# Causal attention with two products a head, one maximum over two banks, and banks handed out by hand

## The chip, the cores and the metric

The kernel runs on one core of one Trainium2 chip. The metric is the device time of one execution in microseconds (us). Engines in the text are those of the profile: PE (matrix products) with PEld (its weight loads), DVE (vector), ACT (scalar functions), POOL, and SP, which here only starts transfers. Each engine works through its own queue in order.

## The reference, cut to what matters

A sequence of 2048 rows of 128 numbers goes through four layers, each added to its own input. The first is a linear recurrence with a gate, the second a choice of one expert out of eight, the third causal attention with 16 heads of 8 numbers each, and the fourth six rounds of windowed attention and a gated feed-forward layer. The change touches the third:

```python
qkv = x @ W_qkv + b_qkv                       # x is normalised first
q, k, v = ...                                 # 16 heads of 8 numbers
scores = einsum('bhqd,bhkd->bhqk', q, k) * D ** (-0.5)
scores = where(tril, scores, -inf)
probs = softmax(scores, axis=-1)
out = einsum('bhqk,bhkd->bhqd', probs, v)
return out @ W_o + b_o
```

## The kernel before

**Layout.** Rows are worked in 4 groups of 512 (`NG`, `GW`), heads in 4 groups of 4 (`NGRP`). A head has a stripe of 32 partitions: its 8 numbers stand there three times, and the last 8 partitions carry other things (below). Four heads fill the 128 partitions, so that their products, 32 partitions high each, can run side by side on PE.

**Precision.** The scores are computed from bfloat16 pieces whose sum is nearly the float32 number. q is cut into three bfloat16 pieces (`project`, L617): the rounded value, the rounded rest, and the rest of that. They are the three planes of the tile `qT`. The key (`keys`, L468) is cut into three pieces as well, but these stand in one plane `kT`, one piece in each of the three 8-partition parts of the stripe. One product of a 32-partition stripe sums a piece of q times all three pieces of k; three products, accumulated in one PSUM bank (512 float32 per partition), give the score (`products`, L630).

**What a key costs.** For each of the 4 row groups and 4 head groups (16 times), `keys` runs a matmul into bank `pk`, ACT `k` (the rounded key), DVE `krest` (the rest), POOL `k` (a product with a 0/1 column) and POOL `kT` (a difference). `project` runs, for each of 16 blocks, a matmul into `pq`, ACT `qT`, DVE `qrest`, POOL `qT` as a cast and POOL `qT` as a difference.

**Two passes.** Softmax needs each row's maximum first. `maxima` (L636) computes the scores with rows on the partitions, up to 512 keys at a time, for two heads in a *half*: the products go into two banks, in the last chunk a small matmul adds the causal mask, and DVE takes the maximum of each bank (`mx`). When a block (one head group, 512 rows) is done, POOL cuts the negated maxima into pieces, and PE and DVE put them into the spare partitions of plane 0 of `qT` (`finish`, L682). Against ones in the key's spare partitions, they subtract the maximum inside the product. `attend` (L703) then computes the scores again, with keys on the partitions, and ACT takes the exponential straight from the bank into `ex`; on the diagonal POOL zeroes the future (`whole`, L746), and PE multiplies with the values into `av`.

**Order.** `attention` (L898) pairs a unit of `attend` for block b with a unit of `maxima` for a later block. A unit is four heads and is done in two halves; a half issues the products of two maxima heads and two attention heads, then the two exponentials, then PE's `av` products of an earlier unit (`weigh_due`), then the two maxima. Where the maxima are behind, `catch_up` (L883) puts a unit of maxima alone, four heads at once; where they are far enough ahead, a unit of `attend` goes alone. All this is order of issue. `InOrder` (L57) pins every PE, DVE, ACT and POOL instruction behind the one issued before it on that engine:

```python
def run(*args, **kw):
    return self._tc.keep_in_program_order(call(*args, **kw))
```

**Banks.** PSUM has 8 banks: one for `av`, seven for everything else, as seven buffers of one pool (L560). A new tile waits until its buffer's last reader is done.

**The front.** Before and beside the first blocks, `front` (L485) runs the recurrence, the experts and the keys. They are generators, merged by written due times (`Merge`, L72). For the experts DVE writes `own`, the rows of one expert, eight times a row group, and PE multiplies each (`py`); before every layer a normalisation goes DVE, POOL (`ln_r`), DVE (`ln_h`), PE (`ln_pt`), ACT (`hT`). `keys` is called for one head group (L466) or for three in a row, and issues all of a key without a break.

Of the kernel before, what the change touches and what calls it, by code (L numbers as in the profile page):

```python
# [93 lines left out]

class Kernel:
# [27 lines left out]
    def norm_transposed(self, pool, psum, x, g, hT):  # L123

        mv = pool.tile([P, G, 2], F32, name="ln_mv")
        for j in range(G):
            st = pool.tile([P, 6], F32, name="ln_st")
            self.dve.bn_stats(st, x[:, g * G + j, :])
            self.dve.bn_aggr(mv[:, j, :], st)
        var = pool.tile([P, G], F32, name="ln_var")  # L130
        self.dve.tensor_scalar_add(var, mv[:, :, 1], EPS)
        r = pool.tile([P, G], F32, name="ln_r")
        self.rsqrt(r, var)
        yield 3.2
# [7 lines left out]
        self.act.copy(hT, pt)  # L142
        yield 2.3
# [54 lines left out]
    def load3(self, w):  # L198
        nc, a = self.nc, self.a
        wqk = w.tile([P, 2, NGRP, P], F32, name="wqk")  # L200
        nc.sync.dma_start(wqk, a["wqk1"])
        bqk = w.tile([P, 4, NGRP], F32, name="bqk")
# [57 lines left out]
    def ssm_inputs(self, pool, psum, x, g, into, f1, gate, xsT):  # L260

        w4, vec, bt, ct = self.w1
        cpg = GW // CL
        hT = pool.tile([P, GW], F32, name="hT", tag="t")
        yield from self.norm_transposed(pool, psum, x, g, hT)
        px = psum.tile([P, GW], F32, name="px", tag="b")
        self.pe.matmul(px, lhsT=w4[:, 0, :], rhs=hT, start=True, stop=True)
        xs_g = xsT[:, g * GW : (g + 1) * GW]
        self.dve.tensor_copy(xs_g, px)
        yield 3.0  # L270
        for c in range(2):
            pb = psum.tile([P, GW], F32, name="pb", tag="b")
            self.pe.matmul(pb, lhsT=bt[:, c, :], rhs=xs_g, start=True, stop=True)
            fg = f1[:, :, c, g * cpg : (g + 1) * cpg].rearrange("p l k -> p k l")
            pb = pb.rearrange("p (k l) -> p k l", l=CL)
            if c == 0:
                self.act.activation(fg, pb, AF.Copy, scale=into)
            else:
                self.dve.tensor_scalar_mul(fg, pb, into)
# [7 lines left out]
        self.act.activation(gate[:, g * G : (g + 1) * G, :], pg, AF.Silu)  # L287

# [53 lines left out]
    def ssm_out(self, pool, psum, x, g, gate, po, u):  # L342
# [11 lines left out]
        for j in range(G):  # L354
            self.act.activation(sq[:, j, :], po[:, j, :], AF.Square, accum_out=ss[:, j : j + 1])
        yield 0.9
# [8 lines left out]
        self.act.copy(uT, pu)  # L365
        yield 1.0
# [6 lines left out]
        for j in range(G):  # L373
            xt = x[:, g * G + j, :]
            self.dve.scalar_tensor_tensor(xt, pr[:, j, :], r[:, j : j + 1], xt, ALU.mult, ALU.add)

    def experts(self, pool, psum, x, g):
# [27 lines left out]
        for j in range(G):  # L407
            act.activation(
                ex[:, j, :], pl[:, j, :], AF.Exp, bias=mx[:, 1, j : j + 1], accum_out=prob[:, j : j + 1]
            )  # L410
        idi = pool.tile([P, G], I32, name="idi")
# [19 lines left out]
        for e in range(EXPERTS):  # L431
            yield 0.7
            own = pool.tile([P, GW], F32, name="own", bufs=4)
            dve.scalar_tensor_tensor(own, pi, float(e), hT, ALU.is_equal, ALU.mult)
            yield 0.4
# [8 lines left out]
        for j in range(G):  # L444
            act.activation(y[:, j, :], py[:, j, :], AF.Relu, scale=prob[:, j : j + 1])
        yield 1.7
# [5 lines left out]
    def keys_values(self, pool, psum, x, g, hT3, kT, va):  # L452
# [11 lines left out]
        )  # L464
        yield 1.3
        yield from self.keys(pool, psum, g, hT3, kT, [0])  # L466

    def keys(self, split, psum, g, hT3, kT, grps):  # L468
        wqk, bqk, wv, wo = self.w3
        hg = hT3[:, g * GW : (g + 1) * GW]  # L470
        for grp in grps:
# [8 lines left out]
            self.dve.scalar_tensor_tensor(rest, pk, bqk[:, 1, grp : grp + 1], one, ALU.add, ALU.subtract)  # L480
            self.gps.tensor_scalar_mul(two, rest, bqk[:, 3, 1:2])
            self.gps.tensor_tensor(kT[:, grp, g * GW : (g + 1) * GW], rest, two, ALU.subtract)
# [71 lines left out]
    def stages123(self, x, x3):  # L554
        nc, tc, a = self.nc, self.tc, self.a
        with ExitStack() as ctx:
# [4 lines left out]
            psum_s = ctx.enter_context(tc.tile_pool(name="s3s", bufs=7, space=PSUM))  # L561
            pe, dve, act, gps = self.pe, self.dve, self.act, self.gps

            class banks:
                @staticmethod
                def tile(shape, dtype, name, tag=None):
                    return psum_s.tile(shape, dtype, name=name, tag="sc")

# [3 lines left out]
            make_kT = lambda: keep.tile([P, NGRP, T], BF16, name="kT3", tag="kT3")  # L572
# [44 lines left out]
            def project(b):  # L617
                grp, qc = blocks[b]
                q = qs[b] = pool.tile([P, 3, GW], BF16, name="qT3", bufs=4)
                pq = bank("pq")  # L620
                pe.matmul(
                    pq, lhsT=wqk[:, 0, grp, :], rhs=hT[:, qc * GW : (qc + 1) * GW], start=True, stop=True
                )
                rest = pool.tile([P, GW], F32, name="qrest")
                act.activation(q[:, 0], pq, AF.Identity, bias=bqk[:, 0, grp : grp + 1])
                dve.scalar_tensor_tensor(rest, pq, bqk[:, 0, grp : grp + 1], q[:, 0], ALU.add, ALU.subtract)
                gps.tensor_copy(q[:, 1], rest)
                gps.tensor_tensor(q[:, 2], rest, q[:, 1], ALU.subtract)

            def products(heads):  # L630
                for i in range(3):
                    for product in heads:
                        product(i)


            def maxima(b):  # L636
# [6 lines left out]
                for j in range(G):  # L643
# [5 lines left out]
                    def part(pr, ch, qt=qt, mx=mx, chunks=chunks, j=j):  # L649
                        c, wd = chunks[ch]  # L650
                        n = len(chunks)
                        scs, heads = [], []
                        for h in (2 * pr, 2 * pr + 1):
                            sc = bank("sc1")
                            scs.append((h, sc))

                            def product(i, r=slice(32 * h, 32 * h + 32), sc=sc):
                                pe.matmul(
                                    sc[:, :wd], lhsT=q[r, i, j * P : (j + 1) * P], rhs=kT[r, grp, c : c + wd],
                                    start=i == 0, stop=i == 2 and ch < n - 1,  # L660
# [21 lines left out]
                def finish():  # L682
# [3 lines left out]
                    dve.tensor_tensor(q[:, 0], q[:, 0], pt, ALU.add)  # L686

# [15 lines left out]
            def attend(b):  # L703
# [15 lines left out]
                for kt in range(last + 1):  # L719
# [3 lines left out]
                    def part(pr, kt=kt, lo=lo):  # L723
# [4 lines left out]
                        for h in (2 * pr, 2 * pr + 1):  # L728
# [3 lines left out]
                            def product(i, r=slice(32 * h, 32 * h + 32), sc=sc):  # L732
                                pe.matmul(
                                    sc[:, lo:], lhsT=kT[r, grp, kt * P : (kt + 1) * P],
                                    rhs=q[r, i, lo:], start=i == 0, stop=i == 2,
# [4 lines left out]
                        def rest():  # L740
                            for h, sc in scs:
                                act.activation(ex[:, h, lo:], sc[:, lo:], AF.Exp)

# [22 lines left out]
                def close():  # L766
# [8 lines left out]
                    def back():  # L775
                        pt = bank("pta").rearrange("p (j h s) -> p j h s", h=4, s=32)
# [13 lines left out]
                        )  # L790
                        if grp == (NGRP - 1 if qc != left else NGRP - 2):
# [4 lines left out]
            def out_a(g):  # L796
# [4 lines left out]
                act.copy(aoT, pt)  # L801

                def out_b():
# [7 lines left out]
                    dve.tensor_tensor(xg, x[:, g * G : (g + 1) * G, :], po, ALU.add)  # L811
                    if g == left:
# [15 lines left out]
            def norm(g, mv, r):  # L828
# [8 lines left out]
                for i in range(2):  # L837
                    rs = slice(64 * i, 64 * i + 64)
                    act.copy(self.s4_in[rs, g * GW + i : (g + 1) * GW + i], pt[rs])

# [709 lines left out]
def _layouts(x):  # L1550
# [18 lines left out]
    bqk = np.zeros((4, NGRP, 4, 32), f)  # L1569
    for i in range(3):  # L1570
# [3 lines left out]
        if i:  # L1574
# [3 lines left out]
    bqk[1, ..., 3 * HD1 : 3 * HD1 + 3] = 1.0  # L1578
    got["wqk1"] = wqk.reshape(P, 2, NGRP, P)
    got["bqk1"] = bqk.reshape(4, NGRP, P).transpose(2, 0, 1)  # L1580
# [35 lines left out]
```

## Time and profile before

| | us |
|---|---|
| median of 3 runs (2319.01 to 2319.07) | 2319.02 |
| the profiled execution, its own time | 2321.57 |
| its span | 2319.6 |

Stages of the span, in us of busy time. They are cut at about where the first score products start (190.6), shortly after the last key is done (268.5), and where the fourth layer begins (783):

| from - to | length | PE | DVE | ACT | POOL | PE clock |
|---|---|---|---|---|---|---|
| 0 - 140 | 140 | 89.53 | 96.78 | 44.58 | 44.74 | 0.82 |
| 140 - 194 | 54 | 39.77 | 34.19 | 13.71 | 28.02 | 0.84 |
| 194 - 275 | 81 | 66.90 | 56.62 | 27.54 | 43.62 | 0.85 |
| 275 - 640 | 365 | 334.63 | 275.47 | 210.94 | 45.38 | 0.97 |
| 640 - 783 | 143 | 128.83 | 78.30 | 91.54 | 22.94 | 0.96 |
| 783 - 2319.6 | 1536.6 | 1468.36 | 1332.99 | 1249.83 | 1206.81 | 0.98 |

How to read it: an engine is busy while one of its instructions runs; matmuls overlap one another, so PE's busy time also covers the fill and drain of a product. The clock is the share of full speed that PE was granted. Nearly every instruction carries the line of the helper `InOrder` (L67), so groups are told apart by their tiles: `sc<-kT,qT` is a product of `maxima` (key columns stream through), `sc<-qT,kT` one of `attend`. Names are those of the output and inputs, and `x12` counts instructions. A float32 matmul appears as two instructions. In the chain of waits each line is a stretch of the work that ended last: its start, its length, and what ran.

### The profile page before, as it was taken

How to read it: one execution, taken by the hardware profiler on the slowest of the kernel's cores; microseconds unless marked ns; L12 is line 12 of the kernel's file. 1: busy time of each engine (PE TensorE's matmuls, PEld its weight loads, DVE VectorE, ACT ScalarE, POOL GpSimd, SP SyncE). 2: the span in 40 equal slices, each digit the busy share in tenths (PEclk: the TensorE clock that was granted, in tenths of full speed). 3: DMA queues.
4: the chain of work that ended last, by engine and by line, in shares of the span. 5: the costliest groups of instructions: out<-in, count | busy, mean ns of one | idle time of the engine just before them, and what ended most of it. 6: DMA issues, size and time to landing. Idle time of an engine off the chain costs nothing.

```text
span 2319.6 us, 62002 instructions
## 1 busy us (share of the span) xinstructions
PE 2128.0 (92%) x26188; PEld 1233.9 (53%) x26188; DVE 1874.4 (81%) x2808; ACT 1638.1 (71%) x3219; POOL 1391.5 (60%) x2122
## 2 busy tenths in 40 slices
PE   4777988999999779999999999999999999999997
PEld 2654323333333346666666666666666666666654
DVE  6667677777766489999899988998999899998963
ACT  3322445566656578888888888888888888888881
POOL 4235411100011489988788878887888887887850
PEclk8787989999999979999999999999999999999998
DMA  2000000000000100000000000000000000000000
GB/s 78 1 1 1 2 2 2 2 2 2 2 2 2 68 2 20 4 20 2 20 11 23 2 20 11 22 2 20 11 22 2 20 9 3 2 2 2 2 6 14
DMA packets 14135, 25.38 MB, mean 11 GB/s; under 512 B 1657, under 2 KB 10530, under 8 KB 13090
## 3 DMA queue, kind: packets, MB, share of 16 engines
q1 hardware_dynamic: 13276, 20.97, 2.8%
q8 instruction: 206, 3.38, 0.6%
q14 instruction: 71, 0.58, 0.1%
q10 hardware_dynamic: 582, 0.46, 0.1%
HBM read 20.37 MB, written 1.05 MB: 9 GB/s over the span
## 4 chain that ended last, share of the span: by engine, by line
PE 64%; DVE 19%; ACT 8%; issue 4%; POOL 3%; DMA 0%; DVEq 0%; POOLq 0%; ACTq 0%; SPq 0%
PE big L67 45%; PE sc L67 9%; PE av L67 5%; DVE mx L67 4%; DVE rot_a L67 3%; DVE rot_b L67 2%; ACT sq L67 2%; ACT L67 1%; ACT ge L67 1%; DVE at L67 1%; ACT zs L67 1%; PE py L67 1%; ACT ex L67 1%; DVE act L67 1%; DVE ss L67 1%
## 5 line engine op out<-in xcount | busy, mean ns | idle before, releaser
L67 ACT ACTIVATE sm<-sm,mx,rn 128x64 f32<-128x64 f32 x1536 | 519.2, 430 | 0.3
L67 DVE TENSOR_REDUCE mx<-sc 128x1 f32<-128x512 f32 (+3 forms) x640 | 355.0, 604 | 125.5 <-PE sc L67 118.6
L67 POOL TENSOR_TENSOR rot_a<-rot_a,rot_b 128x1024 f32<-128x1024 f32 x192 | 454.6, 2368 | 0.1
L67 ACT ACTIVATE ex<-sc 128x512 f32<-128x512 f32 (+3 forms) x640 | 302.6, 536 | 204.1 <-PE sc L67 200.8
L67 PE MATMUL big<-wqk,s 128*128 128x512 f32 x768 | 369.2, 604 | 15.0 <-DVE rot_b L67 10.2
L67 PE MATMUL big<-zs,vo 128*128 128x256 f32 x1536 | 366.9, 382 | 0.3 <-ACT zs L67 0.3
L67 PEld LDWEIGHTS big<-zs,vo 128*128 128x128 f32 x1536 | 280.6, 190 | 88.3 <-issue 56.8
L67 DVE TENSOR_TENSOR rot_a<-big,tab 128x1024 f32<-128x1024 f32 x192 | 233.5, 1216 | 47.1 <-ACT sq L67 36.4
L67 PE MATMUL sc<-qT,kT 32*128 32x512 bf16 (+3 forms) x1920 | 248.4, 351 | 24.6 <-DVE mx L67 16.3
L67 ACT ACTIVATE sq<-big 128x1024 f32<-128x1024 f32 x192 | 197.4, 1028 | 76.0 <-PE big L67 46.1
L67 ACT COPY zs<-big 128x1024 f32<-128x1024 f32 x192 | 192.3, 1006 | 64.3 <-PE big L67 64.3
L67 PE MATMUL sc<-kT,qT 32*128 32x512 bf16 (+3 forms) x1920 | 232.4, 359 | 1.6 <-DVE krest L67 0.5
L67 DVE TENSOR_REDUCE ss<-sq 128x16 f32<-128x1024 f32 x192 | 229.8, 1198 | 1.4
L67 DVE TENSOR_TENSOR rot_b<-big,tab 128x1024 f32<-128x1024 f32 x192 | 230.0, 1198 | 0.3 <-POOL rot_a L67 0.3
L67 PE MATMUL big<-at,xw 32*128 32x512 f32 x1536 | 206.2, 624 | 3.9 <-DVE rot_b L67 1.7
L67 PEld LDWEIGHTS big<-wqk,s 128*128 128x128 f32 x768 | 135.7, 192 | 137.0 <-issue 125.6
L67 PE MATMUL big<-ident,rot_a 128*128 128x128 f32 x1536 | 198.9, 276 | 6.2 <-POOL rot_a L67 3.6
L67 PEld LDWEIGHTS big<-ident,rot_a 128*128 128x128 f32 x1536 | 176.6, 142 | 50.3 <-issue 23.5
L67 POOL TENSOR_SCALAR_AFFINE_SELECT ex<-ex 128x512 f32<-128x512 f32 x64 | 40.8, 638 | 269.8 <-ACT ex L67 269.6
L67 POOL TENSOR_TENSOR sm<-sm,su 128x1024 f32<-128x1024 f32 x96 | 183.1, 1907 | 23.4 <-DVE su L67 22.2
L67 PE MATMUL av<-ex,va 128*32 128x256 f32 (+1 forms) x2432 | 180.5, 377 | 5.0 <-POOL ex L67 3.7
L67 POOL TENSOR_TENSOR rot_a<-rot_a,rn 128x1024 f32<-128x1024 f32 x96 | 182.7, 1904 | 0.2
(236 smaller groups left out, 3342.4 us busy)
## 6 DMA issues: line engine op xcount, KB each, us to landing
wqk<-in_L_ffn_Wqkv SPq DMA_DIRECT2D x12, 512.0 KB, 4.9
wvo<-in_wvo SPq DMA_DIRECT2D x6, 1024.0 KB, 4.9
w<-in_L_ffn_W SPq DMA_DIRECT2D x6, 341.0 KB, 7.5
x<-in_L_attn_hidden_states SPq DMA_DIRECT2D x4, 256.0 KB, 4.3
out<-act SPq DMA_DIRECT2D x4, 256.0 KB, 2.3
rot<-in_rot SPq DMA_DIRECT2D x1, 960.0 KB, 7.0
w<-in_L_ffn_W SPq DMA_DIRECT2D x12, 64.0 KB, 1.9
qks<-in_qks SPq DMA_DIRECT2D x6, 128.0 KB
```

Source lines behind the costliest of these rows:

```text
L67: return self._tc.keep_in_program_order(call(*args, **kw))
```

## The change

- **Two products.** q is cut into two planes instead of three. Plane 0 holds the first piece in 24 of the stripe's 32 partitions and the negated maxima in the last 8; plane 1 holds the second piece in the 24 and the third in the last 8. The keys get two planes as well: plane 1 is the old `kT` with the rounded key once more in its last 8 partitions, where it meets the third piece; plane 0 is made from plane 1 by one more ACT instruction, with a scale and a bias column (it clears the last 8 partitions and sets the ones). Products `i` = 0, 1 use plane `i` of both. `project` gains an ACT copy with a scale, and its POOL cast becomes a POOL product with a column.
- **One maximum for two heads.** The two heads of a `maxima` half take two neighbouring banks; after both masks, one DVE instruction reduces both.
- **Banks.** The seven banks are one PSUM tile. `Banks` keeps a list of free banks in the order in which their last reader was issued; `tile()` takes the first, `pair()` the pair (0,1), (2,3) or (4,5) whose later bank stands earliest. `free()` calls are added behind every last reader.
- The host-side column table `bqk` grows from 4 to 5 rows.

```diff
+class Banks:
+    def __init__(self, tile):
+        self._tile, self._free, self._held = tile, list(range(tile.shape[1])), {}
+    def _hold(self, ap, *banks):
+        for k in banks:
+            self._free.remove(k)
+        self._held[id(ap)] = ap, banks
+        return ap
+    def tile(self, shape, dtype, name, tag=None):
+        k = self._free[0]
+        ap = self._tile[:, k]
+        return self._hold(ap if len(shape) == 2 else ap.rearrange("p (j c) -> p j c", c=shape[2]), k)
+    def pair(self):
+        at = self._free.index
+        ks = [k for k in range(0, self._tile.shape[1] - 1, 2) if k in self._free and k + 1 in self._free]
+        k = min(ks, key=lambda k: max(at(k), at(k + 1)))
+        return self._hold(self._tile[:, k : k + 2], k, k + 1)
+    def free(self, ap):
+        self._free.extend(self._held.pop(id(ap))[1])
...
 def keys(self, split, psum, g, hT3, kT, grps):
...
             self.dve.scalar_tensor_tensor(rest, pk, bqk[:, 1, grp : grp + 1], one, ALU.add, ALU.subtract)
+            psum.free(pk)
             self.gps.tensor_scalar_mul(two, rest, bqk[:, 3, 1:2])
-            self.gps.tensor_tensor(kT[:, grp, g * GW : (g + 1) * GW], rest, two, ALU.subtract)
+            cols = slice(g * GW, (g + 1) * GW)
+            self.gps.tensor_tensor(kT[:, 1, grp, cols], rest, two, ALU.subtract)
+            self.act.activation(
+                kT[:, 0, grp, cols], kT[:, 1, grp, cols], AF.Identity, bias=bqk[:, 3, 3:4], scale=bqk[:, 3, 2:3]
+            )
             yield 0.9
...
-            psum_s = ctx.enter_context(tc.tile_pool(name="s3s", bufs=7, space=PSUM))
...
+            banks = Banks(psum.tile([P, 7, GW], F32, name="sc"))
...
-            make_kT = lambda: keep.tile([P, NGRP, T], BF16, name="kT3", tag="kT3")
+            make_kT = lambda: keep.tile([P, 2, NGRP, T], BF16, name="kT3", tag="kT3")
...
 def project(b):
-                q = qs[b] = pool.tile([P, 3, GW], BF16, name="qT3", bufs=4)
+                q = qs[b] = pool.tile([P, 2, GW], BF16, name="qT3", bufs=4)
...
-                act.activation(q[:, 0], pq, AF.Identity, bias=bqk[:, 0, grp : grp + 1])
-                dve.scalar_tensor_tensor(rest, pq, bqk[:, 0, grp : grp + 1], q[:, 0], ALU.add, ALU.subtract)
-                gps.tensor_copy(q[:, 1], rest)
-                gps.tensor_tensor(q[:, 2], rest, q[:, 1], ALU.subtract)
+                one, two = (pool.tile([P, GW], BF16, name=f"q{i}") for i in range(2))
+                act.activation(one, pq, AF.Identity, bias=bqk[:, 0, grp : grp + 1])
+                dve.scalar_tensor_tensor(rest, pq, bqk[:, 0, grp : grp + 1], one, ALU.add, ALU.subtract)
+                banks.free(pq)
+                act.activation(q[:, 0], one, AF.Copy, scale=bqk[:, 3, 2:3])
+                gps.tensor_scalar_mul(two, rest, bqk[:, 4, 0:1])
+                gps.tensor_tensor(q[:, 1], rest, two, ALU.subtract)
 
 def products(heads):
-                for i in range(3):
+                for i in range(2):
...
 def part(pr, ch, ...):          # of maxima
-                        for h in (2 * pr, 2 * pr + 1):
-                            sc = bank("sc1")
+                        pair, heads = banks.pair(), []
+                        for h in (2 * pr, 2 * pr + 1):
...
-                            for h, sc in scs:
+                            for h in range(2):
                                 if ch == n - 1:
-                                    pe.matmul(sc[:, wd - P : wd], lhsT=self.ident16, rhs=mask, start=False, stop=True)
-                                dve.reduce_max(mx[:, h, ch : ch + 1], sc[:, :wd], axis=AX.X)
+                                    pe.matmul(
+                                        pair[:, h, wd - P : wd], lhsT=self.ident16, rhs=mask, start=False, stop=True
+                                    )
+                            dve.reduce_max(mx[:, 2 * pr : 2 * pr + 2, ch], pair[:, :, :wd], axis=AX.X)
+                            banks.free(pair)
```

More of the change, by code (lines that the diff above doesn't have):

```diff
@@ L142, in norm_transposed @@
         self.act.copy(hT, pt)
+        psum.free(pt)
         yield 2.3
@@ L201, in load3 @@
         nc.sync.dma_start(wqk, a["wqk1"])
-        bqk = w.tile([P, 4, NGRP], F32, name="bqk")
+        bqk = w.tile([P, 5, NGRP], F32, name="bqk")
         nc.sync.dma_start(bqk, a["bqk1"])
@@ L269, in ssm_inputs @@
         self.dve.tensor_copy(xs_g, px)
+        psum.free(px)
         yield 3.0
@@ L274, in ssm_inputs @@
             fg = f1[:, :, c, g * cpg : (g + 1) * cpg].rearrange("p l k -> p k l")
-            pb = pb.rearrange("p (k l) -> p k l", l=CL)
+            pv = pb.rearrange("p (k l) -> p k l", l=CL)
             if c == 0:
-                self.act.activation(fg, pb, AF.Copy, scale=into)
+                self.act.activation(fg, pv, AF.Copy, scale=into)
             else:
-                self.dve.tensor_scalar_mul(fg, pb, into)
+                self.dve.tensor_scalar_mul(fg, pv, into)
+            psum.free(pb)
         yield 14.0
@@ L287, in ssm_inputs @@
         self.act.activation(gate[:, g * G : (g + 1) * G, :], pg, AF.Silu)
+        psum.free(pg)
     def ssm_chunks(self, co, ys, zy, yt):
@@ L355, in ssm_out @@
             self.act.activation(sq[:, j, :], po[:, j, :], AF.Square, accum_out=ss[:, j : j + 1])
+        psum.free(po)
         yield 0.9
@@ L365, in ssm_out @@
         self.act.copy(uT, pu)
+        psum.free(pu)
         yield 1.0
@@ L375, in ssm_out @@
             self.dve.scalar_tensor_tensor(xt, pr[:, j, :], r[:, j : j + 1], xt, ALU.mult, ALU.add)
+        psum.free(pr)
     def experts(self, pool, psum, x, g):
@@ L410, in experts @@
             )
+        psum.free(pl)
         idi = pool.tile([P, G], I32, name="idi")
@@ L434, in experts @@
             dve.scalar_tensor_tensor(own, pi, float(e), hT, ALU.is_equal, ALU.mult)
+            if e == EXPERTS - 1:
+                psum.free(pi)
             yield 0.4
@@ L445, in experts @@
             act.activation(y[:, j, :], py[:, j, :], AF.Relu, scale=prob[:, j : j + 1])
+        psum.free(py)
         yield 1.7
@@ L464, in keys_values @@
         )
+        psum.free(pv)
         yield 1.3
@@ L560, in stages123 @@
             psum = ctx.enter_context(tc.tile_pool(name="s3p", bufs=1, space=PSUM))
-            psum_s = ctx.enter_context(tc.tile_pool(name="s3s", bufs=7, space=PSUM))
             pe, dve, act, gps = self.pe, self.dve, self.act, self.gps
[L564 to L567, printed above, removed]
+            banks = Banks(psum.tile([P, 7, GW], F32, name="sc"))
             wqk, bqk, wv, wo = self.w3
@@ L651, in part, with product @@
                         n = len(chunks)
-                        scs, heads = [], []
+                        pair, heads = banks.pair(), []
                         for h in (2 * pr, 2 * pr + 1):
-                            sc = bank("sc1")
-                            scs.append((h, sc))
-                            def product(i, r=slice(32 * h, 32 * h + 32), sc=sc):
+                            def product(i, r=slice(32 * h, 32 * h + 32), sc=pair[:, h % 2]):
                                 pe.matmul(
-                                    sc[:, :wd], lhsT=q[r, i, j * P : (j + 1) * P], rhs=kT[r, grp, c : c + wd],
-                                    start=i == 0, stop=i == 2 and ch < n - 1,
+                                    sc[:, :wd], lhsT=q[r, i, j * P : (j + 1) * P], rhs=kT[r, i, grp, c : c + wd],
+                                    start=i == 0, stop=i == 1 and ch < n - 1,
                                 )
@@ L686, in finish @@
                     dve.tensor_tensor(q[:, 0], q[:, 0], pt, ALU.add)
+                    banks.free(pt)
                 yield 0, finish, None
@@ L733, in product @@
                                 pe.matmul(
-                                    sc[:, lo:], lhsT=kT[r, grp, kt * P : (kt + 1) * P],
-                                    rhs=q[r, i, lo:], start=i == 0, stop=i == 2,
+                                    sc[:, lo:], lhsT=kT[r, i, grp, kt * P : (kt + 1) * P],
+                                    rhs=q[r, i, lo:], start=i == 0, stop=i == 1,
                                 )
@@ L742, in rest @@
                                 act.activation(ex[:, h, lo:], sc[:, lo:], AF.Exp)
+                                banks.free(sc)
                         return heads, rest
@@ L775, in back @@
                     def back():
-                        pt = bank("pta").rearrange("p (j h s) -> p j h s", h=4, s=32)
+                        held = bank("pta")
+                        pt = held.rearrange("p (j h s) -> p j h s", h=4, s=32)
                         for j in range(G):
@@ L790, in back @@
                         )
+                        banks.free(held)
                         if grp == (NGRP - 1 if qc != left else NGRP - 2):
@@ L801, in out_a @@
                 act.copy(aoT, pt)
+                banks.free(pt)
                 def out_b():
@@ L811, in out_b @@
                     dve.tensor_tensor(xg, x[:, g * G : (g + 1) * G, :], po, ALU.add)
+                    banks.free(po)
                     if g == left:
@@ L839, in norm @@
                     act.copy(self.s4_in[rs, g * GW + i : (g + 1) * GW + i], pt[rs])
+                banks.free(pt)
             def stream(make):
@@ L1567, in _layouts @@
     wqk = np.zeros((P, 2, NGRP, 4, 32), f)
-    bqk = np.zeros((4, NGRP, 4, 32), f)
-    for i in range(3):
+    bqk = np.zeros((5, NGRP, 4, 32), f)
+    for i in range(4):
         s = slice(i * HD1, (i + 1) * HD1)
@@ L1573, in _layouts @@
         bqk[0:2, ..., s] = x["L1_attn_b_qkv"][: 2 * P].reshape(2, NGRP, 4, HD1)
-        if i:
+        if i in (1, 2):
             bqk[2, ..., s] = bqk[1, ..., s]
@@ L1577, in _layouts @@
     bqk[3, 1, :, 2 * HD1 : 3 * HD1] = 1.0
-    bqk[1, ..., 3 * HD1 : 3 * HD1 + 3] = 1.0
+    bqk[3, 2, :, : 3 * HD1] = 1.0
+    bqk[3, 3, :, 3 * HD1 : 3 * HD1 + 3] = 1.0
+    bqk[4, 0, :, 3 * HD1 :] = 1.0
     got["wqk1"] = wqk.reshape(P, 2, NGRP, P)
-    got["bqk1"] = bqk.reshape(4, NGRP, P).transpose(2, 0, 1)
+    got["bqk1"] = bqk.reshape(5, NGRP, P).transpose(2, 0, 1)
     got["bv1"] = x["L1_attn_b_qkv"][2 * P :].reshape(1, P)
```

## The prediction

> **What bounds the kernel now.** I read the windows of busy time by stage first. The fourth layer (783 to the end) issues nothing that the change touches, so I go only into 140 to 783. There I took one full block of attention, 16 units of `maxima` and 16 of `attend`, which repeats three times to a hundredth:
>
> ```profile
> core 0: us, PE busy (x) PEld busy (x) DVE busy (x) ACT busy (x) POOL busy (x), PEclk, DMA share, GB/s
> 498.70:551.06 52.36, 49.31 (x666) 17.21 (x658) 39.77 (x73) 32.93 (x66) 5.43 (x13) 1.00 0.01 2
> 551.06:603.42 52.36, 49.31 (x666) 17.23 (x658) 39.77 (x73) 32.93 (x66) 5.40 (x12) 1.00 0.01 2
> ```
>
> PE is busy 94%, DVE 76%, ACT 63%. PE bounds the block, but DVE isn't far. The groups of instructions of the first of these windows say with what:
>
> ```profile
> L67 DVE TENSOR_REDUCE mx<-sc 128x1 f32<-128x512 f32 x53 | 33.7, 684 | 5.9 <-PE sc L67 5.1
> L67 ACT ACTIVATE ex<-sc 128x512 f32<-128x512 f32 x52 | 28.1, 600 | 15.2 <-PE sc L67 15.2
> L67 PE MATMUL sc<-qT,kT 32*128 32x512 bf16 x156 | 23.7, 376 | 2.0 <-DVE mx L67 1.6
> L67 PE MATMUL sc<-kT,qT 32*128 32x512 bf16 x156 | 20.9, 378 | 0.1
> ```
>
> The chain of waits of the same stretch gives the beat: a half is 0.82 us of score products (12 of them, three rounds of four) and 0.57 us of `av`. It also shows what breaks the beat: runs of DVE maxima of 3 us, and once a block the chain of a new q through POOL.
>
> ```profile
> 498.00 0.62 POOL qT L67
> 498.70 1.16 POOL qT L67
> 499.86 0.60 POOL ex L67
> 500.50 0.42 PE av L67 x8
> ...
> 509.78 3.08 DVE mx L67 x5
> 512.86 0.04 issue
> 512.91 0.80 PE sc L67 x9
> 513.71 0.57 PE av L67 x8
> 514.28 0.82 PE sc L67 x12
> ```
>
> The front is another matter. There the chain of waits runs through the keys, on POOL, straight into the experts' `own`:
>
> ```profile
> 141.03 0.75 ACT k L67
> 141.81 0.77 DVE krest L67
> 142.67 1.58 POOL k L67
> 144.32 1.15 POOL kT L67
> 145.48 1.56 POOL k L67
> 147.11 1.16 POOL kT L67
> 148.30 0.75 DVE krest L67
> 149.05 2.39 DVE own L67 x4
> ```
>
> **The change, part by part.**
>
> *A third of the products goes.* In the beat, successive rounds start 0.215 us apart (the timeline has them at 527.01, 527.23, 527.45), and the 0.17 us after the last round stays. A half falls from 0.82 + 0.57 = 1.39 to 1.17 us. From 275 to 640 there are 412 exponentials and about 420 maxima, 832 heads, so 208 rounds of four are dropped; at a mean width near 460 columns that is 208 x 0.19 = 40 us. From 640 to 783, with 184 and about 100, it is 71 x 0.17 = 12 us, and before 275 about 5 us.
>
> *One maximum for two.* Two single ones take 1.29 us back to back (two-instruction rows of the DVE timeline). The double one isn't in the trace. The width rows give its slope: 285 ns for 128 columns, 684 for 512, so 684 + 512 x 1.04 = 1216 ns. A sum over 1024 (`ss<-sq`, from SBUF) takes 1198 ns, and `rot_b<-big`, which reads two banks, 1198 ns. Bounds 1.14 (the pitch of singles, 0.61, plus 512 columns) and 1.29 (nothing merged); I take 1.2. DVE's 39.8 us of a block become about 37 and PE's 49.3, less 32 rounds of 0.2, become 43, so DVE stands at 86% of PE's work instead of 81%. In a wide half the three engines are then nearly level: PE 1.17, DVE 1.2, ACT 1.09 for its two exponentials. The next to be late is DVE.
>
> *The order of the banks.* Today a half takes four of seven banks in turn, so its last product waits for the first maximum of the half before it. At 520.27 to 522.65 the products of one half take 2.38 us instead of 0.82 for that reason, and two or three such places make the block 52.36. Its beats (32 x 1.39), eight masks of 0.2 and 2.1 for transposes and `pq` are 48.2, about 47.5 with the narrow halves taken off. With `pair()` the maxima alternate over pairs and may lag a full half more, while the exponentials rotate through the three others. Gain between 0 (DVE keeps its own pace) and the whole 4.8 us a block. I take 2, since DVE has less air than before; over 365 / 52.36 = 7 blocks that is 14 us.
>
> *The new q.* POOL's cast (612 ns) becomes a product with a column. The same form in `keys` takes 1567 ns, so POOL's chain before the diagonal's `ex` is 0.96 us longer. It is on the chain of waits in five blocks: +5 us. Elsewhere the queue behind it, POOL's `ex` and maxima pieces, has slack. The added ACT copy, 0.6 to 0.78 us by ACT's 512-column rows, lies beside PE's `av` and score products; ACT has 19 us of air in a block. Without that cover it would cost 0.7 x 16 = 11 us. It waits for nothing but the instruction before it.
>
> So the attention alone gains 40 - 5 + 14 = 49 us up to 640. After 640, units of `attend` often go alone and ACT's four exponentials (2.06 us) already outlast PE; of the 12 us I count 8. Sum: **-57**.
>
> *The key's second plane.* This is the added wait. `keys` ends with an ACT instruction that reads POOL's `kT`, and ACT's queue is in order. Whatever comes next on ACT stands behind DVE `krest` and both POOL steps: the next key's `k`, an exponential, a new q. Today four keys in a row are paced by POOL alone, 1.57 + 1.15 + gaps = 2.78 us each. Then a key starts only when the one before is wholly done: 0.86 (`krest` and gap) + 1.65 + 1.15 + 0.05 + 0.78 (the new instruction, priced as ACT `k`, which also has two column operands; a plain copy is 0.59) + 0.75 (`k`) + 0.05 = 5.3 us. Place by place:
> - Four keys at 141: the fourth `krest` at 141.8 + 3 x 5.3 = 157.7 instead of 148.3. `own` is queued behind it on DVE and is on the chain: +9.
> - Four keys at 168: by the same sum 184.9 instead of 175.5, again with `own` behind: +9.
> - One key at 196: ACT's next work comes at 205.6: 0.
> - Three keys at 208.7, with eight exponentials and a q between them: `ln_h` is queued on DVE behind `qrest`, which needs ACT `qT`. That ACT instruction comes at about 229.7 instead of 219.5: +9 on `ln_h`.
> - One key at 235: the exponentials behind it wait until 240.7, POOL's `ex` at 239.8 slips to 241.5: +2.5.
> - Three keys at 256.3: the exponential of 261.0 stands behind all three and comes at about 274.5; PE runs out of exponentials' banks at about 264: +10.
>
> Sum 40 us. What could hide it is only air between these places; bounds are 15 (only the two groups at 141 and 168, partly overlapped) and 60. The front's own share of dropped products, 5 us, is taken off: **+35**.
>
> *The table, the free calls, the start of layer four.* `bqk` grows by a quarter of 8 KB, loaded once long before use: 0. The seven banks as one tile could make the first tile of layer four wait for the last reader of all banks; ACT's last exponential is done by 782 and PE's first product there (784.05) waits for ACT `s`: 0.
>
> Net: -57 + 35 = **-22 us** on the profiled execution (2321.57 own time, 2319.6 span). That execution stands 2.6 us above the median of the runs, and I move the difference over unchanged: 2319.0 - 22 = **2297 us**.
>
> [...]
>
> **The rivals.**
> *The wait in `keys` outweighs the products.* Place: 141 to 275. Its price is 60 where every exponential behind a key is exposed and PE's clock falls, and the gain is 45 where DVE takes back what the banks give: +15, 2334 us. It decides from the point where the price passes the gain. For it: in the front the chain already runs through POOL `kT`. Against: some of the places overlap.
> *The wait is hidden.* If the front absorbs all but 15 us, with 5 off for its products, the sum is -57 + 10 = -47: 2272 us. For it: ACT is busy only 13.7 of 54 us there. Against: what is idle in ACT is the chain itself.
> *DVE becomes the bound.* At 1.29 us a pair (no saving) DVE still needs 39.8 us a block, and with its waits for masks (often 1.03 us idle before a masked maximum, by the DVE timeline) the block ends near 49. That is 3.4 x 7 = 24 us gained, 8 more later, against 35: +3, 2322 us.
> *The one tile doesn't let banks go singly.* If products waited for all readers, a half would last 0.6 + 1.2 + 0.15 = 1.95 us against 52.36 / 32 = 1.64 now: 0.31 x 320 = +99, with +35 about 2450 us. Against: one tile `kT` is written in slices beside products that read other slices, without a wait.
>
> **How the numbers follow.** The likeliest, 2297, has 0.48, with its own range of 2283 to 2312 (gain 48 to 65, price 28 to 43). The hidden wait has 0.22, the heavy wait 0.14, DVE's bound 0.13, the tile 0.03. A measurement of this kernel tells about 0.2%, 4.6 us. Faster takes the first two, and 0.03 of DVE's: 0.73. The rest of DVE's is 0.08 same and 0.02 slower, which with the heavy wait and the tile makes slower 0.19. The range reaches to both middle rivals and to part of the heavy wait: 2266 to 2328.
>
> **What would show it.** Right: 2560 score products, 320 double maxima near 1.2 us, a full block near 46 us with PE still above DVE; in the front, `krest` of four keys 5.3 us apart, `own` 9 us late twice, the last key done near 304 instead of 268. Wrong: keys at 2.8 us still (then the time is near 2270), or a block near 50 with DVE above 95% busy, or PE waiting for ACT's exponentials in each half.

## The result and the profile after

The changed kernel takes **3124.88 us** (median of 4 runs, 3122.36 to 3128.68) against 2319.05 for the kernel before: a ratio of 1.347, with an interval of 1.345 to 1.349. That is slower by more than a third. The profiled execution has a span of 3124.5 us.

Windows of busy time of the kernel after, cut where the first score products start and where attention ends:

```profile
core 0: us, PE busy (x) PEld busy (x) DVE busy (x) ACT busy (x) POOL busy (x), PEclk, DMA share, GB/s
140.00:323.00 183.00, 112.37 (x394) 81.99 (x395) 60.91 (x164) 25.64 (x61) 42.71 (x30) 0.53 0.00 0
323.00:1587.00 1264.00, 733.71 (x5479) 214.71 (x5481) 402.20 (x511) 350.00 (x712) 126.12 (x211) 0.51 0.01 2
1590.00:3124.00 1534.00, 1465.84 (x18720) 935.20 (x18720) 1331.65 (x1621) 1249.44 (x2381) 1204.17 (x1767) 0.99 0.04 12
```

The first score products start at 323.4 instead of 190.6 (+133). The fourth layer's first product starts at 1590.35 instead of 784.05 (+806), so attention lost 673 more. The fourth layer itself takes as long as before. In attention no engine is near full: PE 58%, DVE 32%, ACT 28%. Added up, that is 118%; in the block of before, the same three numbers add up to 233%. The engines hardly work beside each other any more. And PE's clock is 0.51 on the mean of those 1264 us.

The chain of waits after shows one half of a unit:

```profile
1118.04 1.09 PE sc L67 x8
...
1119.21 1.09 ACT ex L67 x2
...
1120.33 1.24 DVE mx L67
1121.57 0.04 issue
1121.61 1.09 PE sc L67 x8
...
1122.73 1.09 ACT ex L67 x2
...
1123.85 1.24 DVE mx L67
```

Eight products, then two exponentials, then one double maximum, then the next products, each starting within 0.1 us of the end of the one before it. From 1118.04 to 1121.61 are 3.57 us; the beat of before was 52.36 / 32 = 1.64. The waits over the whole of attention (323 to 1587) say who stands behind whom:

```profile
engine line waited for: us in total, times, longest us
ACT ex L67 <- PE sc L67: 743.6, 280, 11.1
...
PE sc L67 <- DVE mx L67: 393.3, 299, 2.6
DVE mx L67 <- ACT ex L67: 354.7, 156, 7.4
DVE mx L67 <- PE sc L67: 340.3, 143, 7.9
```

The third of these lines is the odd one: a maximum waits for an exponential, 156 times. They read different banks, and neither writes one. In the front the same happens to the experts, whose `pi` and `py` are banks too (chain of waits after):

```profile
187.39 2.09 PE sc L67 x8
...
189.50 0.70 DVE own L67
190.20 0.04 issue
190.25 2.09 PE sc L67 x8
...
192.36 0.70 DVE own L67
```

DVE writes the next `own` only when PE has finished with the one before it, 2.8 us a step.

### The profile page after: what moved, and what is told of

The parts are those of the page before. It is cut to its first block, busy times and chain, and to the rows that moved or that the text cites. A ratio compares the mean times of both kernels' runs of the same rounds, so it can differ in the third digit from the quotient of the medians.

```text
span 3124.5 us, 59598 instructions
## 1 busy us (share of the span) xinstructions
PE 2391.6 (77%) x24908; PEld 1285.3 (41%) x24908; DVE 1860.6 (60%) x2488; ACT 1663.1 (53%) x3251; POOL 1404.6 (45%) x2122
## 4 chain that ended last, share of the span: by engine, by line
PE 51%; DVE 21%; ACT 15%; issue 4%; POOL 2%; DMA 0%; DVEq 0%; ACTq 0%; POOLq 0%; SPq 0%
PE big L67 33%; PE sc L67 17%; DVE mx L67 11%; ACT ex L67 9%; DVE rot_a L67 2%; DVE rot_b L67 2%; ACT sq L67 1%; DVE at L67 1%; PE av L67 1%; ACT L67 1%; ACT ge L67 1%; ACT zs L67 1%; DVE act L67 1%; DVE ss L67 1%; ACT kT L67 1%
## 5 line engine op out<-in xcount | busy, mean ns | idle before, releaser
L67 DVE TENSOR_REDUCE mx<-sc 128x2 f32<-128x1024 f32 (+4 forms) x324 | 342.2, 1061 | 713.8 <-ACT ex L67 354.7
L67 PE MATMUL sc<-kT,qT 32*128 32x512 bf16 (+3 forms) x1280 | 259.8, 544 | 372.5 <-DVE mx L67 304.4
L67 PE MATMUL av<-ex,va 128*32 128x256 f32 (+1 forms) x2432 | 290.0, 582 | 0.6 <-POOL ex L67 0.6
L67 PE MATMUL sc<-qT,kT 32*128 32x512 bf16 (+3 forms) x1280 | 261.0, 547 | 32.0 <-DVE mx L67 22.0
L67 PEld LDWEIGHTS <-qT 32*128 32x128 bf16 x1280 | 65.2, 103 | 534.2 <-issue 530.9
```

## The experiments

Three explanations went into the first four runs. T: banks that are slices of one PSUM tile make engines wait for one another, whichever bank each of them uses. Q: the new pieces of q and k, with their longer chains over POOL and ACT, take the time. O: the order in which banks are taken does.

### One tile alone, and its banks apart

The kernel before, with three products, single maxima and its own q and keys, but with banks taken in the order of release: once from one tile, once from seven.

```diff
-            psum_s = ctx.enter_context(tc.tile_pool(name="s3s", bufs=7, space=PSUM))
+            banks = Banks(psum.tile([P, 7, GW], F32, name="sc"))                             # onetile
+            banks = Banks([psum.tile([P, w, GW], F32, name=f"sc{i}") for i, w in enumerate((1, 1, 1, 1, 1, 1, 1))])     # order
...
                                 dve.reduce_max(mx[:, h, ch : ch + 1], sc[:, :wd], axis=AX.X)
+                                banks.free(sc)
```

> The kernel before with one thing changed: its seven banks are slices of one PSUM tile, handed out in the order of release. Three products, single maxima and the keys are as before. Theory T (the tile): an access to any bank of the tile waits for what other engines were issued earlier on the other banks, so that in each half PE's products, ACT's exponentials and DVE's maxima run one after another. A half is then about 1.5 (three rounds at half clock, as PE idles) + 1.09 + 1.29 = 3.9 us instead of the changed kernel's 3.5: 3200 to 3300 us. Theory Q (the new ACT step in the keys and the double maximum hold the queues up): neither is in here, so 2300 to 2340. Theory O (the order of release makes PE wait for the bank that comes free last): also slow, and then the next run, with the same order, must be slow too.

> As the run onetile, but the seven banks are seven PSUM tiles; the order of release is the same. T: 2285 to 2325, the kernel before less whatever the order gives (at most 34 us by the waits of PE for the maxima of the half before). O: above 3000. Q: 2300 to 2340, which does not tell it from T here.

Measured: one tile 3292.61 us (ratio 1.418, 1.415 to 1.422); seven tiles 2315.83 us (0.998, 0.996 to 1.000). The instructions are the same, and so is the list from which free banks are taken. The tile alone is worth 977 us, and Q has no part in that: neither kernel has the new pieces. The chain of waits of the one-tile kernel has the same ring; at a masked chunk even the two heads of a half take turns:

```profile
1015.36 1.48 PE sc L67 x12
...
1016.92 1.09 ACT ex L67 x2
...
1018.05 0.28 PE sc L67
...
1018.35 0.57 DVE mx L67
...
1018.97 0.28 PE sc L67
...
1019.27 0.57 DVE mx L67
```

The second head's mask (1018.97) goes into a bank of its own, yet starts only when DVE is done with the first head's. With seven tiles the longest waits of ACT and DVE in attention (188 to 778) are those of a kernel whose engines overlap:

```profile
engine line waited for: us in total, times, longest us
...
ACT ex L67 <- PE sc L67: 170.9, 236, 6.5
DVE mx L67 <- PE sc L67: 120.8, 115, 3.3
```

A maximum stands behind an exponential twice there, for 3.7 us in all, against 354.7 us in the kernel after. T holds; O falls as well, since both kernels take banks in the same order.

What these runs show is the cost of a wait that covers a tile of seven banks: ACT and DVE overlap in the kernel with seven tiles, on different banks, and take turns with one tile, where a maximum waits 422.9 us for exponentials, 155 times (317 to 1755).

### The whole change with its banks apart

Everything as in the change, but the tile is cut: into tiles of 2, 2, 1, 1, 1 banks (`apart`) and of 4 and 3 (`twotiles`). Pairs come from the first ones; once the maxima have begun, single banks come from the others where one is free.

```diff
-            banks = Banks(psum.tile([P, 7, GW], F32, name="sc"))
+            banks = Banks([psum.tile([P, w, GW], F32, name=f"sc{i}") for i, w in enumerate((2, 2, 1, 1, 1))])   # apart
+            banks = Banks([psum.tile([P, w, GW], F32, name=f"sc{i}") for i, w in enumerate((4, 3))])            # twotiles
```

> The whole change (two products, second plane of the keys, one maximum over two banks), but the seven banks are five PSUM tiles: two of two banks for the pairs, three of one bank. pair() chooses between the two double tiles, tile() prefers the single ones once pairs are in use. T: the forecast without the tile holds, 2297 (2266 to 2328), PE's clock above 0.95, DVE's maxima no longer wait for exponentials. Q: above 2700. O: above 2700, as the order is nearly that of the change.

> The whole change, but the seven banks are two PSUM tiles: four banks for the pairs and three for the rest. T: in attention DVE's maxima no longer wait for ACT's exponentials, but PE waits for both; a half is about 1.0 + 1.24 + 0.1 = 2.3 us instead of 3.5, so some 380 us less than the changed kernel: 2550 to 2800. Q or O: as the changed kernel, 3100 to 3150.

Measured: `apart` 2388.85 us (1.030, 1.027 to 1.033), `twotiles` 2777.6 us (1.197, 1.194 to 1.200). The more banks share a tile, the more time: 2389, 2778, 3125. In `twotiles` the maxima's tile is not that of the exponentials, as long as single banks are free, and in the waits of its attention no maximum stands behind an exponential any more, only behind PE (424.6 us). So 736 of the 806 us go with the seven-bank tile: 94 of them ahead of the first score product, which comes at 229.5 in `apart` instead of 323.4, and 643 between it and the fourth layer (853.2 instead of 1590.4). But `apart` was forecast at 2297: the other parts of the prediction, which this kernel measures with at most two banks in a tile, missed by 92 us as well. The remaining runs look for those.

### Two products, and the wait in the keys

`two` has the two products, the two key planes and the new q, with the buffers and the single maxima of before. `defer` issues a key's second plane one key later, behind the next key's first ACT instruction:

```diff
             self.gps.tensor_tensor(kT[:, 1, grp, cols], rest, two, ALU.subtract)
-            self.act.activation(
-                kT[:, 0, grp, cols], kT[:, 1, grp, cols], AF.Identity, bias=bqk[:, 3, 3:4], scale=bqk[:, 3, 2:3]
-            )
+            if last is not None:
+                plane(last)
+            last = grp
             yield 0.9
+        yield 2.0
+        plane(last)
```

> The kernel before with the two products, the two planes of kT and the new q alone: seven separate buffers in turn and single maxima as before. By the forecast's sums (the products' 40 + 5 + 8, less 5 for POOL's longer q, less the price of 40 in the keys; nothing for the order of the banks) the time is about 2319 - 8 = 2311 us. If the blocks lose what the products give, as the five-tile kernel did between 275 and 640 (clock 0.79), only the keys' price stays: 2340 to 2370 us. If the keys' wait is hidden: 2271 us. The key pitch is 5.2 us in any case.

> As the kernel with two products alone, but ACT makes a key's second plane one key later, after the next key's first ACT instruction, so ACT doesn't stand on POOL's kT. If that wait costs what the forecast said, the key pitch is 2.8 us again, the last key is done near 270 instead of 305 and the time is 35 to 45 us below the kernel with two products alone. If the front is late for another reason (the plane's ACT time itself, the clock), the two stand within 10 us.

Measured: `two` 2326.28 us (1.003, 1.002 to 1.004), `defer` 2300.09 us (0.992, 0.990 to 0.994). The wait in the keys costs 26 us, less than the 35 to 45 that were expected. In the timeline of ACT in `two` it stands as forecast:

```profile
139.60 0.79 ACT L67 ACTIVATE k<-pk,bqk 128x512 bf16<-128x512 f32 x1
144.12 0.81 ACT L67 ACTIVATE kT<-kT,bqk 128x512 bf16<-128x512 bf16 x1 [3.73 <-POOL kT L67]
144.84 0.76 ACT L67 ACTIVATE k<-pk,bqk 128x512 bf16<-128x512 f32 x1
149.32 0.81 ACT L67 ACTIVATE kT<-kT,bqk 128x512 bf16<-128x512 bf16 x1 [3.72 <-POOL kT L67]
```

ACT stands 3.7 us on POOL, and keys are 5.2 us apart. In `defer` POOL's `kT` come at 142.45, 145.24 and 148.01, 2.8 us apart, and the last key's at 274.34 instead of 299.99 (267.31 in the kernel before).

### The chain of a new q

`qdve` is `defer` with one instruction on another engine:

```diff
-                gps.tensor_scalar_mul(two, rest, bqk[:, 4, 0:1])
+                dve.tensor_scalar_mul(two, rest, bqk[:, 4, 0:1])
```

> As the last one, with one more edit: DVE instead of POOL makes the rounded rest of q (about 0.5 us instead of 1.57), so the chain of a new q is DVE 0.75 + 0.5, POOL 1.16. If the longer POOL chain, and the half clock of TensorE after it, is what keeps a block at 50 us, a block falls to 45 to 47 us and the time by 15 to 35 us. If the chain costs only its own 0.96 us in five blocks, it gains 5 us; if DVE is the bound, it loses up to 8 (16 x 0.5).

Measured: 2288.72 us (0.987, 0.985 to 0.988), 11 us below `defer`, between the 5 and the 15 to 35 that were named. On DVE the instruction takes 0.49 us. A full block, from ACT `q` to ACT `q`, in the windows of `two`, then of `qdve`:

```profile
522.57:571.20 48.63, 43.83 (x534) 13.60 (x533) 38.87 (x72) 33.53 (x67) 6.26 (x12) 1.00 0.01 2
```

```profile
490.36:537.85 47.49, 43.81 (x534) 13.72 (x533) 39.35 (x73) 33.54 (x68) 4.74 (x11) 1.00 0.01 1
```

The full block loses 1.14 us, about the difference of POOL's 1.57 and DVE's 0.49, at a clock of 1.00 in both (in `defer` it takes 48.63 as well). Most of the 11 us comes from two shorter blocks, which fall from 40.24 to 35.07 and from 44.53 to 40.43 us. In both the clock was 0.85 and is 1.00. The windows of the first, in `defer`, then in `qdve`:

```profile
360.24:400.48 40.24, 33.61 (x358) 9.39 (x358) 29.01 (x56) 21.13 (x43) 5.04 (x10) 0.85 0.01 1
```

```profile
363.30:398.37 35.07, 29.28 (x358) 9.36 (x356) 29.28 (x57) 21.13 (x43) 3.52 (x9) 1.00 0.01 2
```

The same 358 products, at a lower clock behind the longer chain. So part of the lowered clock was the q chain's. In the full block DVE still holds PE up, in the chain of waits of `qdve`:

```profile
502.90 4.19 DVE mx L67 x7
507.14 0.59 PE sc L67 x5
...
513.25 4.19 DVE mx L67 x7
517.49 0.59 PE sc L67 x5
```

Seven single maxima in a row, twice a block, with PE's products waiting behind the last.

### The double maximum

`pairs` has three products, q and keys as before, and double maxima on tiles of 2, 2, 1, 1, 1 banks. `pairfront` differs from it only in how banks are drawn ahead of attention (two users share a tile only where nothing else is free), and `grouped` is `pairfront` with two single maxima on each two-bank tile.

```diff
-                                dve.reduce_max(mx[:, h, ch : ch + 1], sc[:, :wd], axis=AX.X)
+                            dve.reduce_max(mx[:, 2 * pr : 2 * pr + 2, ch], pair[:, :, :wd], axis=AX.X)   # pairs, pairfront
+                            for h in range(2):                                                            # grouped
+                                dve.reduce_max(mx[:, 2 * pr + h, ch : ch + 1], pair[:, h, :wd], axis=AX.X)
...
-        k = self._free[0] if self._first else min(self._free, key=lambda k: (k in double, self._free.index(k)))
+        beside = lambda k: any(k in ks and not set(ks) <= set(self._free) for ks, _ in self._pairs)
+        k = min(self._free, key=lambda k: (self._first and beside(k), k in double, self._free.index(k)))          # pairfront, grouped
```

> Three products, keys and q as before; only the double maximum, with its two-bank tiles (tiles of 2, 2, 1, 1, 1 banks). By the forecast the double maximum takes 1.2 us for two of 0.684 and PE stays the bound: within 2305 to 2320 us. If banks held two by two cost more than DVE gains (a pair is freed only when both heads are reduced, and in the front the two banks of a tile wait for each other), 2325 to 2350 us. The sum of this kernel's difference and that of the one with two products alone should be near the +70 us of the five-tile kernel if the parts add.

> As the kernel with double maxima and three products (2370.5 us), but ahead of the attention the tiles are drawn so that two of them share a two-bank tile only where no other bank is free. If the experts' products and own, which share one there, are what makes the front late (first score product at 213.4 instead of 190.6), 15 to 23 us less: 2347 to 2356. If the front is late for another reason: 2365 to 2372.

> As the last one, but each two-bank tile is reduced by two single maxima, one a head. If what costs is that two banks are taken and freed together, the time is within 8 us of the last one. If it is the length of the double maximum (1.22 us before either bank is free, and 0.6 us later for the last of a block), 15 to 30 us less than the last one.

Measured: `pairs` 2370.54 us (1.022, 1.020 to 1.024), `pairfront` 2342.42 us (1.008, 1.005 to 1.011), `grouped` 2352.02 us (1.013, 1.012 to 1.015). The double maximum takes 1.22 us, as forecast, and yet the kernel is 51 us slower. That is more than the 2325 to 2350 that were named as its bad case. Part of it is T again, in the front: `own` and PE took turns in a two-bank tile, and drawn apart the first score product comes at 194.1 instead of 213.4. By the medians that is worth 28 us, by the profiled executions 16 (the four of `pairfront` spread from 2334 to 2352, and its profile is of the slowest). The rest is in the blocks. Windows of a full block, `pairfront` and then `grouped`:

```profile
517.81:572.06 54.25, 49.99 (x662) 16.28 (x662) 37.72 (x40) 33.05 (x67) 5.42 (x12) 0.97 0.01 2
```

```profile
519.73:574.29 54.56, 49.99 (x661) 16.26 (x658) 39.60 (x72) 33.03 (x66) 5.42 (x12) 0.97 0.01 2
```

With seven tiles (`order`) a full block takes 51.70 (ACT `qT` at 497.61, 549.31 and 601.00). Merging the two maxima saves 1.9 us of DVE's time and 0.3 of the block's; taking the banks in twos costs 2.9, at a clock of 0.97 where `order` has 1.00. `grouped` is 9.6 us above `pairfront` by the medians, a little more than the 8 allowed for (the two profiled executions are level), and not 15 to 30 below it, so the length of the double maximum isn't the cause. In the chain after a new q, `grouped` shows one place where the time goes, since exponentials then rotate through three banks:

```profile
523.19 0.60 POOL ex L67
524.26 0.87 PE sc L67 x12
525.13 1.82 ACT ex L67 x4
527.03 0.62 ACT avs L67
528.20 0.80 PE sc L67 x9
```

In the chain of `order` the same place has one exponential of 0.60 us. That the three banks are the reason is argued from this chain, and wasn't tried by itself; nor was DVE's piece of q with three products.

### The parts together

`mended` is the whole change with five tiles, the banks of the front drawn as in `pairfront`, the deferred plane and DVE's piece of q. `best` is `qdve` with seven separate tiles in the order of release.

```diff
# mended, against the change
-            banks = Banks(psum.tile([P, 7, GW], F32, name="sc"))
+            banks = Banks([psum.tile([P, w, GW], F32, name=f"sc{i}") for i, w in enumerate((2, 2, 1, 1, 1))])
...
+            if last is not None:
+                plane(last)
...
+                dve.tensor_scalar_mul(two, rest, bqk[:, 4, 0:1])
```

```diff
# best, against qdve
-            banks = Banks(ctx.enter_context(tc.tile_pool(name="s3s", bufs=7, space=PSUM)))
+            banks = Banks([psum.tile([P, w, GW], F32, name=f"sc{i}") for i, w in enumerate((1, 1, 1, 1, 1, 1, 1))])
```

> The whole change with five tiles (2388.9 us), the front's banks as in the two kernels before this one, the key's plane one key later, and DVE for the rounded q. If the parts add: 2388.9 - 26 (plane) - 11 (q) - 15 to 23 (front) = 2329 to 2337 us. If the double maximum pays once there are only two products and DVE is nearer to the bound, at or below 2289.

> Two products, the key's plane one key later, DVE for the rounded q, seven separate tiles taken in the order of release, single maxima. The last version without the order of release took 2288.7 us; in the block its runs of seven maxima on DVE (4.19 us, twice) hold PE up. If the order of the banks relaxes that, as the forecast said (2 us a block), 2270 to 2282 us; if it gives what it gave the kernel before (0.2%), 2282 to 2288; if DVE itself is the bound, no change.

Measured: `mended` 2330.75 us (1.003, 1.001 to 1.005; ten runs, 2319 to 2333), in the median inside what the parts add up to. `best` 2301.06 us (0.991, 0.989 to 0.993): the order of release, worth 3.7 us to the kernel before, costs 12 here, where no loss had been expected, though a full block of its profiled execution is shorter (47.04). That execution took 2292.88, and the other three runs 2300 to 2302; where they lose isn't seen in a profile, and stays open. The fastest kernel is `qdve`, 1.3% below the kernel before.

The traces of `mended` and `apart` also show what the double maximum costs with two products. Of the edits between the two, only DVE's piece of q issues anything in a full block, since the keys are done by then. One of three full blocks, in `apart`, then in `mended`:

```profile
571.88:626.19 54.31, 48.56 (x534) 13.09 (x534) 37.49 (x40) 33.64 (x68) 6.33 (x12) 0.84 0.01 1
```

```profile
525.99:573.19 47.20, 42.24 (x534) 12.62 (x534) 37.27 (x41) 33.65 (x67) 4.82 (x11) 1.00 0.01 1
```

The three take 53.49, 54.31 and 50.47 us in `apart`, at clocks of 0.84, 0.84 and 0.93, and 49.86, 47.20 and 47.48 in `mended`, at 0.93, 1.00 and 1.00. So in the full blocks of `apart` most of the loss was the long q chain with a lowered clock behind it. It takes the pairs as well: `two` has the same chain with single maxima, and its block is 48.63 us at 1.00. That fits the sums: `pairs` and `two` lose 51 and 7 us, `apart`, with both, 69. At full clock the block is as long as `qdve`'s 47.49: the two banks taken together cost it nothing there, and the 2 us that merging saves DVE gain nothing. What `mended` loses against `qdve` comes elsewhere: its q of the same block is 14 us late at 315, 33 at 476 and 35 at 573, and its fourth layer starts 41 us later.

## Why the prediction was wrong, point by point

**The seven banks as one tile: 0.** This step failed. It looked only at the start of layer four, and there it was right (1534 us after, 1536 before). Ahead of that layer the tile cost 736 us against `apart`, by the profiled executions 643 in attention and 94 in the front. The mechanism stood among the rivals, with the sum 0.6 + 1.2 + 0.15 = 1.95 us a half. Two terms were missing. It took the readers to be free of one another, so ACT's two exponentials (1.09) weren't in the ring; and it took PE at full clock, while in the ring the clock is half (products 1.09 instead of 0.63 in `qdve`, +0.46). 1.95 + 1.09 + 0.46 = 3.50, and 3.57 was measured. The argument against it, that `kT` is written in slices beside products that read others, was about a tile outside PSUM and didn't carry over. What could have been read from the profile before: a block of 52.36 us holds 33.7 us of maxima and 28.1 of exponentials, 61.8 in all, so they read banks at the same time, and the diff puts those banks into one tile. That was a condition to price in full.

**The key's second plane: +35.** Right in kind and nearly in size. In `two`, `own` comes 7.9 us late, then 16.4 in all (forecast 9 and 18), the last key 32.7 late (about 36). In time, the move in `defer` was worth 26 us: attention takes some of the delay back, and `defer`'s last key is still 7 us late.

**A third of the products goes: 40 + 5 + 8.** The beat was right: a full block of `two` takes 48.63 us, where the forecast's 46 without its 2 for the order of the banks makes 48. Its counts of maxima, about 420 and 100, were 441 and 114, which is worth under 2 us. The front's 5 us was wrong. In `defer` the q that ACT made at 286.61 before comes at 299.64, 13 us late: the last key is still 7 us late, and the clock from 194 to 275 is 0.75 instead of 0.85. From there to the fourth layer 33 us are gained, where 40 + 8 - 5 were forecast, and 20 remain. So `defer` ended at 2300, not 2271.

**The new q: +5.** The size was right: moving the piece from 1.57 us on POOL to 0.49 on DVE took 1.14 us off a block, and the forecast had 0.96 for the way from 0.62 to 1.57. The sum over the blocks wasn't: the move was worth 11 us, not 5, and with it the clock from 275 to 640 went from 0.92 to 0.97. Behind the longer chain PE can also lose clock (0.85 in two blocks of `defer`, 0.84 in two full blocks of `apart`, 1.00 with DVE's piece), and the sum had no term for that.

**One maximum for two: 1.2 us.** The duration was right (1.22). That two banks taken and freed together cost 2.6 us a block with three products (54.25 against 51.70) had no term in the sum, nor had the front's tile shared by two users. With two products and the short q chain that cost is gone, and the block of 47.2 us is near the forecast's 46. The rival in which DVE becomes the bound named a block near 49; `two` shows 48.63 with single maxima, but with DVE busy 80% of it and PE 90%, so there the number fits and the bound doesn't.

**The order of the banks: -14.** Mis-sized: 52.36 to 51.70 us a block, 3.7 us in all, and no gain in the median with two products.

**The clock.** The sum of the forecast has no term for it. The trace of before has a stretch in attention where it is low: from 320 to 332 it is 0.54, and eight `av` take 1.01 us instead of 0.57.

```profile
320.00:332.00 12.00, 11.91 (x113) 3.39 (x112) 6.20 (x14) 3.58 (x11) 1.94 (x3) 0.54 0.01 2
```

In the kernel after the clock is at half for 1264 us; in `apart` it is 0.79 from 275 to 640, where it was 0.97 (0.92 in `defer`, 0.88 in `mended`, 0.97 in `qdve`). In the full blocks it was the long q chain, together with the pairs, that pulled `apart` down; for the front and the shorter blocks the parts weren't separated.

**The range.** By its own bounds (gain 48 to 65, price 28 to 43) the likeliest case goes from 2282 to 2314, not from 2283 to 2312. That changes nothing here.

## What to carry to other kernels

Look up what the unit of waiting is before banks are gathered in one tile: with tiles of one bank the three engines overlapped, and with one tile of seven the same instructions took 42% longer, because even readers stood behind each other. Where engines fall into a ring, add all their times, and price PE at the clock that it gets there (half, in the ring here). An instruction whose input comes late from another engine belongs one step later in an in-order queue; here that move alone was worth 26 us.

## What was not expected of the hardware

PE's clock stayed near 0.50 for the whole ring (0.51 on the mean from 323 to 1587), though PE was busy 58% of the time and the waits of its score products for a maximum were 2.6 us at most and for an exponential 3.7. In PE's timeline of the ring, work without a pause (of more than 0.12 us) lasts 2.05 us in the median. Why the clock didn't come back isn't shown. In `defer` it falls in the block that begins at 591.16, right behind a pause of 1.44 us, and in the 40 us before that PE never paused for more than 0.6. The line of PE's timeline with the pause, and the windows around it:

```profile
596.24 0.42 PE L67 MATMUL av<-ex,va 128*32 128x128 f32 x8 [1.44 <-POOL ex L67]
```

```profile
594.00:596.00 2.00, 0.80 (x14) 0.21 (x13) 1.09 (x2) 0.86 (x5) 1.92 (x3) 1.00 0.00 0
596.00:598.00 2.00, 1.76 (x25) 0.69 (x29) 0.00 (x0) 0.27 (x1) 0.78 (x2) 0.64 0.04 8
598.00:600.00 2.00, 2.00 (x27) 0.57 (x18) 0.12 (x1) 2.00 (x5) 0.00 (x0) 0.50 0.00 0
```

A pause of 1.45 us in the block before, up to 547.62, left the clock at 1.00. So of two pauses of nearly the same length one stood ahead of a fall and one didn't; what decides isn't shown.

A reduction over two banks of 512 took 1.22 us, against 2 x 0.684 for two reductions over one.
